# The last layer of a four-layer graph network, computed with the column nodes on the partitions

## The chip, the cores and the metric

The kernel runs on one core of a Trainium2 chip. A core has five engines that run their own instruction streams in order: TensorE (PE in the profile, with its weight loads as PEld), VectorE (DVE), ScalarE (ACT), GpSimd (POOL) and SyncE (SP), which here issues nearly all DMA transfers. The metric is the device time of one execution in microseconds (us), as the median of several runs. A profile comes from one more execution, with its own span.

## The reference

There are 16 batch elements, each with N = 1024 nodes of D = 128 features and a 1024 x 1024 adjacency matrix in fp32, sparse, with values between 0.05 and 1. Four layers follow each other, each as x = x + layer(relu(layernorm(x)), adj). The change touches the last one only, a graph attention layer:

```python
def _L3_gnn_ref(inp, A, W, a):          # inp: relu(layernorm(x)), B x N x 128
    ALPHA, NEG_INF = 0.2, -1e12
    Wh = jnp.matmul(inp, W)
    Wh1 = jnp.matmul(Wh, a[:H, :])       # one number per row node
    Wh2 = jnp.matmul(Wh, a[H:, :])       # one number per column node
    A_ = A + jnp.eye(N)
    e = (Wh1 + jnp.swapaxes(Wh2, 1, 2)) * A_
    e = jnp.where(e >= 0, e, ALPHA * e)
    scores = jnp.where(A_ > 0, e, NEG_INF)
    attention = jax.nn.softmax(scores, axis=2)
    h_prime = jnp.matmul(attention, Wh)
    return jax.nn.elu(h_prime)
```

Layers 0 and 1 average over neighbours; layer 2 scores each edge by a small network. They stay as they are.

## The kernel before

Three "lanes" of work are woven into each other: the edge network of layer 2 for batch b (the main part), the first layers of batch b+1, and the end of batch b-1 (the last update of layer 2 and the whole of layer 3). Each lane is a generator that says with every yield how much of its work is done, and `weave` advances the lane that is furthest behind. The compiler then orders the instructions of each engine. P is 128, T = 8 blocks of 128 nodes, HALF = 512.

```python
            self.work, self.lane = work, lane
            self.homes, self.home = [(f"h{lane}", n_scratch)], 0
            self.psum, self.banks, self.turn_of = psum, banks, 0
        # ...
        def scratch(self, name):
            tag, bufs = self.homes[self.home % len(self.homes)]
            self.home += 1
            return self.work.tile([P, T, P], F32, tag=tag, name=name, bufs=bufs)
        # ...
        def one(self, name):

            tag, bufs = self.banks[self.turn_of % len(self.banks)]
            self.turn_of += 1
            return self.psum.tile([P, HALF], F32, tag=tag, name=name, bufs=bufs)

        def halves(self, name):

            for h in range(NH):
                ps = self.one(f"{name}_{h}").rearrange("p (t d) -> p t d", d=P)
                yield range(h * Q, (h + 1) * Q), ps
```

A lane draws its PSUM tiles with `one`; lane c, which runs layer 3, has a single bank (`own = {"m": ("pre", 2), "a": ("a", 1), "c": ("c", 1)}`), one row buffer (`N_ROW`) and five scratch tiles (`N_SCRATCH`). The helpers for products:

```python
        def by_node(self, hT, w, name):

            for ts, ps in self.halves(f"bn_{name}"):
                for i, t in enumerate(ts):
                    nc.tensor.matmul(ps[:, i], hT[:, t], w, start=True, stop=True)
                yield slice(ts[0], ts[-1] + 1), ps

        def by_feature(self, hT, w, dst, name):

            for ts, ps in self.halves(f"bf_{name}"):
                sl = slice(ts[0], ts[-1] + 1)
                nc.tensor.matmul(ps, w, hT[:, sl], start=True, stop=True)
                nc.scalar.activation(dst[:, sl], ps, AF.Copy)

        def neighbours(self, mat, z, name):

            ps = self.one(f"nb_{name}")[:, :D]
            for k in range(T):
                nc.tensor.matmul(ps, mat[:, k], z[:, k], start=(k == 0), stop=(k == T - 1))
            return ps
```

Layer 3, with the row nodes on the partitions. For each block of 128 rows it loads the rows of adj, forms the scores, takes the exponential, turns the 128 x 1024 weights by eight transposes on PE, copies them out of PSUM, and multiplies them by wh:

```python
        def layer3(self, xt, row, name):

            hT = self.pre_ln(xt, f"3_{name}")
            yield 6
            wh = self.scratch(f"wh_{name}")
            for sl, ps in self.by_node(hT, w3_sb, f"wh_{name}"):
                nc.scalar.activation(wh[:, sl], ps, AF.Copy)
            whT = self.scratch(f"whT_{name}")
            self.by_feature(hT, w3_sb, whT, f"whT_{name}")
            ps = self.one(f"wh1_ps_{name}")
            for t in range(T):
                nc.tensor.matmul(ps[:, t : t + 1], whT[:, t], a3_sb[:, 0:1], start=True, stop=True)
            wh1 = self.small([P, T], "wh1", f"wh1_{name}")
            nc.vector.tensor_copy(wh1, ps[:, :T])
            wh2 = self.scratch(f"wh2_{name}")
            self.by_feature(whT, a2_bc, wh2, f"wh2_{name}")
            wh2 = flat(wh2)
            yield 8

            o = self.scratch(f"o3_{name}")
            rsum = self.small([P, 2, T], "rsum", f"rsum_{name}")
            for t in range(T):
                at = row(t)
                own = at[:, t * P : (t + 1) * P]
                nc.vector.tensor_add(own, own, ident)
                e = flat(self.scratch(f"e_{name}_{t}"))
                nc.vector.scalar_tensor_tensor(
                    e, wh2, wh1[:, t : t + 1], at, op0=OP.add, op1=OP.mult
                )
                self.weights(e, at, rsum[:, 0, t : t + 1], f"{name}_{t}")
                attT = self.scratch(f"attT_{name}_{t}")
                for ks, ps in self.halves(f"attT_ps_{name}_{t}"):
                    for i, k in enumerate(ks):
                        nc.tensor.transpose(ps[:, i], e[:, k * P : (k + 1) * P], ident)
                    nc.scalar.activation(attT[:, ks[0] : ks[-1] + 1], ps, AF.Copy)
                hp = self.neighbours(attT, wh, f"3_{name}_{t}")
                nc.vector.reciprocal(rsum[:, 1, t : t + 1], rsum[:, 0, t : t + 1])
                nc.scalar.activation(o[:, t], hp, AF.Copy, scale=rsum[:, 1, t : t + 1])
                yield 5
            self.sums_seen(rsum, name)
            # ... elu and the addition to xt
```

In the main path `weights` is this (sums are taken beside the mask, without the maximum):

```python
        def weights(self, e, at, total, name):
            nc.vector.scalar_tensor_tensor(e, e, L3_ALPHA, e, op0=OP.mult, op1=OP.max)
            nc.scalar.activation(e, e, AF.Exp)
            nc.vector.scalar_tensor_tensor(
                e, at, 0.0, e, op0=OP.is_gt, op1=OP.mult, accum_out=total
            )
```

Where the rows come from, and how accumulators of layer 2 are started by a product with zeros:

```python
        def acc(self, h, name):

            ps = self.psum.tile([P, HALF], F32, tag=f"acc{h}", name=name)
            nc.tensor.matmul(ps, self.zero16, self.iota2, start=True, stop=True)
            return ps
        # ...
        def last(self, s, b):


            def row(t):
                return flat(
                    self.load(
                        "c", adj[b, t * P : (t + 1) * P, :].rearrange("p (k n) -> p k n", n=P),
                        f"a3_{b}_{t}",
                    )
                )

            lane = self.c
            new = lane.scratch(f"y_{b}")
            for h, dst in enumerate(self.halves_of(new)):
                xT, msgT = self.halves_of(s.pairs[h])
                self.back(xT, s.xT[h])
                yield from lane.update(L - 1, s.xf[h], xT, msgT, dst, f"{b}_{L - 1}_{h}")
            xt = self.back(self.work.tile([P, T, D], F32, tag="x", name=f"xb_{b}"), s.x)
            nc.vector.tensor_add(xt, xt, new)
            yield from lane.layer3(xt, row, f"{b}")
            nc.sync.dma_start(out[b].rearrange("(t p) d -> p t d", p=P), xt)
```

The first layers write the transposed adjacency of each batch to DRAM, for layer 1 and the edge network:

```python
            s.adjT = self.dram.tile([N, N], F32, tag="adjT", name=f"adjT_{b}")
            # ... for each t: load rows, transpose on PE, copy
                nc.sync.dma_start(self.columns(s.adjT, t), turned)
```

Of the kernel before, what the change touches and what calls it, by code (L numbers as in the profile page):

```python
# [9 lines left out]
F32 = mybir.dt.float32  # L10
# [31 lines left out]

MAIN_US = 243.0
FIRST_US = 118.0
LAST_US = 79.0


SPLIT = (0, 1, 0, 0, 1, 0, 1, 0)
# [3 lines left out]
def tile_four_gnn_layers(  # L52
# [88 lines left out]

    half_neg = const.tile([P, T], F32, name="half_neg")
    nc.vector.memset(half_neg, -0.5)
    a2_bc = const.tile([P, P], F32, name="a2_bc")

    slide = const.tile([P, L, 2 * G - 1], F32, name="slide")
    nc.vector.memset(slide, 0.0)
# [9 lines left out]
    def fold_weights():  # L157


        nc.vector.tensor_copy(a2_bc, a3_sb[:, 1:2].to_broadcast([P, P]))  # L160
        signs = slide[:, :, G - 1]
        nc.scalar.activation(signs, we2_sb, AF.Sign)
        nc.vector.tensor_mul(we2_sb, we2_sb, signs)
        nc.vector.tensor_mul(be1_sb, be1_sb, we2_sb)
        nc.scalar.activation(we2_rows, we2_rows, AF.Abs)
        for l in range(L):
            nc.vector.tensor_mul(
                we1_sb[:, l], we1_sb[:, l], we2_rows[:, l, None, :].to_broadcast([P, 2, D])
            )


    unit = const.tile([P, 2, L], F32, name="unit")

    def scale_layer(i):
        for l in range(L):
# [3 lines left out]
    def flat(t):  # L179
        return t.rearrange("p t d -> p (t d)")  # L180
# [4 lines left out]
    class Layers:  # L185
# [8 lines left out]
        def scratch(self, name):  # L194
            tag, bufs = self.homes[self.home % len(self.homes)]
            self.home += 1
            return self.work.tile([P, T, P], F32, tag=tag, name=name, bufs=bufs)

        def small(self, shape, tag, name):
            return self.work.tile(shape, F32, tag=f"{tag}{self.lane}", name=name)  # L200
# [155 lines left out]
            nc.vector.tensor_add(dst, dst, over_t(rows["beta"][:, l], Q))  # L356
            yield 1

        def weights(self, e, at, total, name):

            nc.vector.tensor_scalar(at, at, 0.0, L3_NEG, op0=OP.is_le, op1=OP.mult)
            nc.vector.scalar_tensor_tensor(e, e, L3_ALPHA, e, op0=OP.mult, op1=OP.max)
            nc.vector.tensor_add(e, e, at)
            nmax = self.small([P, 1], "nmax", f"nmax_{name}")
            nc.vector.tensor_reduce(nmax, e, axis=AX.X, op=OP.max, negate=True)
            nc.scalar.activation(e, e, AF.Exp, bias=nmax, accum_out=total)

        def sums_seen(self, rsum, name):
            pass

        def layer3(self, xt, row, name):

            hT = self.pre_ln(xt, f"3_{name}")
            yield 6
            wh = self.scratch(f"wh_{name}")
            for sl, ps in self.by_node(hT, w3_sb, f"wh_{name}"):
                nc.scalar.activation(wh[:, sl], ps, AF.Copy)
            whT = self.scratch(f"whT_{name}")
            self.by_feature(hT, w3_sb, whT, f"whT_{name}")
            ps = self.one(f"wh1_ps_{name}")  # L380
            for t in range(T):
                nc.tensor.matmul(ps[:, t : t + 1], whT[:, t], a3_sb[:, 0:1], start=True, stop=True)
            wh1 = self.small([P, T], "wh1", f"wh1_{name}")
            nc.vector.tensor_copy(wh1, ps[:, :T])
            wh2 = self.scratch(f"wh2_{name}")
            self.by_feature(whT, a2_bc, wh2, f"wh2_{name}")
            wh2 = flat(wh2)
            yield 8

            o = self.scratch(f"o3_{name}")  # L390
# [6 lines that stand above are left out]
                nc.vector.scalar_tensor_tensor(  # L397
                    e, wh2, wh1[:, t : t + 1], at, op0=OP.add, op1=OP.mult
                )
                self.weights(e, at, rsum[:, 0, t : t + 1], f"{name}_{t}")  # L400
                attT = self.scratch(f"attT_{name}_{t}")
                for ks, ps in self.halves(f"attT_ps_{name}_{t}"):
                    for i, k in enumerate(ks):
# [3 lines that stand above are left out]
                nc.vector.reciprocal(rsum[:, 1, t : t + 1], rsum[:, 0, t : t + 1])  # L407
                nc.scalar.activation(o[:, t], hp, AF.Copy, scale=rsum[:, 1, t : t + 1])
                yield 5
            self.sums_seen(rsum, name)  # L410
            neg = self.scratch(f"neg_{name}")
            nc.vector.tensor_scalar(neg, o, 0.0, None, op0=OP.min)
            nc.scalar.activation(neg, neg, AF.Exp)
            nc.vector.scalar_tensor_tensor(o, o, 0.0, neg, op0=OP.max, op1=OP.add)
            nc.vector.scalar_tensor_tensor(xt, o, -1.0, xt, op0=OP.add, op1=OP.add)
# [26 lines left out]
    class Batch:  # L442
# [2 lines left out]

        builds = iter(())

    class Lane(Layers):

        fine = None

        def weights(self, e, at, total, name):
            nc.vector.scalar_tensor_tensor(e, e, L3_ALPHA, e, op0=OP.mult, op1=OP.max)
            nc.scalar.activation(e, e, AF.Exp)
            nc.vector.scalar_tensor_tensor(
                e, at, 0.0, e, op0=OP.is_gt, op1=OP.mult, accum_out=total
            )

        def sums_seen(self, rsum, name):

# [7 lines left out]
    class Edges:  # L470
# [25 lines left out]
        def acc(self, h, name):  # L496

            ps = self.psum.tile([P, HALF], F32, tag=f"acc{h}", name=name)
            nc.tensor.matmul(ps, self.zero16, self.iota2, start=True, stop=True)
            return ps  # L500

        def constants(self):
            con = self.con
# [40 lines left out]
        def scaled(self):  # L544

            con = self.con
            fold_weights()
            self.scale_terms()
            self.slide = con.tile([P, L, 2 * G - 1], F16, name="slide16")
            nc.vector.tensor_copy(self.slide, slide)  # L550

# [97 lines left out]
        def first(self, b):  # L649
# [5 lines left out]
            yield 8  # L655


            s.adjT = self.dram.tile([N, N], F32, tag="adjT", name=f"adjT_{b}")
            has = self.work.tile([P, len(BUCKETS), P], FP8, tag="has", name=f"has_{b}", bufs=1)
            deg = self.work.tile([P, 2, T], F32, tag="deg", name=f"deg_{b}")  # L660
            rdeg = deg[:, 1]
# [452 lines left out]
        def last(self, s, b):  # L1114


            def row(t):
                return flat(
                    self.load(
                        "c", adj[b, t * P : (t + 1) * P, :].rearrange("p (k n) -> p k n", n=P),  # L1120
                        f"a3_{b}_{t}",
                    )
                )

            lane = self.c
            new = lane.scratch(f"y_{b}")
# [3 lines left out]
                yield from lane.update(L - 1, s.xf[h], xT, msgT, dst, f"{b}_{L - 1}_{h}")  # L1130
            xt = self.back(self.work.tile([P, T, D], F32, tag="x", name=f"xb_{b}"), s.x)
            nc.vector.tensor_add(xt, xt, new)
            yield from lane.layer3(xt, row, f"{b}")
            nc.sync.dma_start(out[b].rearrange("(t p) d -> p t d", p=P), xt)

        def run(self):
# [166 lines left out]
    with tc.If(full > 0):  # L1303
        with ExitStack() as stack:
            path = Pairs(stack)
            scale_layer(1)
            with tc.For_i(0, B, 1) as b:
                path.batch(b)

# [31 lines left out]
```

## Time and profile before

| | |
|---|---|
| median of 3 runs | 5564.11 us (5563.31 to 5570.9) |
| profiled span | 5577.4 us, 115653 instructions |
| ACT busy, instructions | 3225.1 us, 7014 |
| POOL busy, instructions | 174.0 us, 137 |
| moved by DMA | 554.68 MB, mean 99 GB/s |
| loads of adjacency rows for layer 3 | 128 of 512 KB, 3.6 us to landing |

The profile counts an engine as busy while an instruction of it runs. For PE the end of a matmul is modelled, so its busy share is not a share of its peak. A group line of the profile gives the line of the kernel, the engine, the operation, the tiles (out<-in), the shapes, the count, then busy time and mean length of one, then the idle time of the engine just before such instructions and what ended it. The chain is found by going back from the last instruction, at each step to what released it.

### The profile page before, as it was taken

Reading aid. Unit: us, or ns where it says so; the run is one execution under the profiler, and the core shown is the slowest. Engines: PE = TensorE matmul, PEld = TensorE weight load, DVE = VectorE, ACT = ScalarE, POOL = GpSimd, SP = SyncE. Lnnn points to the kernel's source line nnn. Section 1 sums busy time; section 2 is a strip of 40 time slices with the busy share of each in tenths; the row PEclk is TensorE's granted clock in tenths of the full one; section 3 lists DMA queues with packets and bytes.
Section 4 is the critical chain, followed back from the end, with each engine's and each line's share of the span. In section 5 each row is a group of like instructions: output and inputs, shape, how many; then the busy total and the mean of one; then the engine's idle time right before and its main releaser. Section 6 shows DMA issues by size and latency. Waiting matters only on the chain.

```text
span 5577.4 us, 115653 instructions
## 1 busy us (share of the span) xinstructions
PE 5156.6 (92%) x46146; PEld 3845.1 (69%) x46146; DVE 4260.5 (76%) x10517; ACT 3225.1 (58%) x7014; POOL 174.0 (3%) x137
## 2 busy tenths in 40 slices
PE   5999999999999999999999999999999999999996
PEld 4676767667677676677767677676766767777665
DVE  3776787877778787787877878678787877878776
ACT  4555564755647555575655647556475665656543
POOL 0000000000000000000000000000000000000000
PEclk8999999999999999999999999999999999999998
DMA  5243324243242433424233242432424334242121
GB/s 174 62 139 93 114 69 136 81 122 97 83 131 66 123 99 96 125 62 129 92 110 110 65 137 82 116 103 79 137 68 124 95 93 132 62 129 88 47 68 41
DMA packets 706355, 554.68 MB, mean 99 GB/s; under 512 B 31248, under 2 KB 636176, under 8 KB 705808
## 3 DMA queue, kind: packets, MB, share of 16 engines
q1 hardware_dynamic: 700704, 545.57, 33.0%
q8 instruction: 364, 5.96, 0.4%
q10 hardware_dynamic: 5104, 1.65, 0.1%
q14 instruction: 183, 1.50, 0.1%
HBM read 446.44 MB, written 100.66 MB: 98 GB/s over the span
## 4 chain that ended last, share of the span: by engine, by line
PE 65%; DVE 16%; ACT 7%; DMA 6%; issue 3%; POOL 3%; SPq 1%; ACTq 0%; POOLq 0%; DVEq 0%
PE pre L916 16%; PE nb L275 9%; PE p L1027 7%; PE msg L1044 6%; DVE val L1005 5%; PE sc L948 4%; PE h L329 3%; PE bb L283 3%; DMA at<-in_adj_dram 3%; PE pn L747 2%; PE pq L780 2%; DVE hid L933 2%; POOL st L230 2%; PE attT_ps L404 2%; PE pm L747 2%
## 5 line engine op out<-in xcount | busy, mean ns | idle before, releaser
L933 DVE SCALAR_TENSOR_TENSOR hid<-pre,hid 128x320 f16<-128x320 f32 (+1 forms) x2048 | 997.4, 505 | 352.6 <-ACT hid L932 342.5
L932 ACT ACTIVATE hid<-pre 128x320 f16<-128x320 f32 (+1 forms) x2048 | 911.2, 453 | 597.2 <-PE pre L916 563.1
L916 PEld LDWEIGHTS <-part 128*128 128x128 f16 x8192 | 753.4, 99 | 411.5 <-issue 198.4
L916 PE MATMUL pre<-on,part 128*128 128x320 fp8e4 (+1 forms) x4096 | 978.9, 311 | 59.6 <-DVE hid L933 55.1
L916 PE MATMUL pre<-om,part 128*128 128x320 fp8e4 (+1 forms) x4096 | 985.4, 310 | 0.0
L1044 PE MATMUL msg<-upd,xf 128*128 128x128 f32 (+3 forms) x3008 | 613.0, 322 | 3.0 <-DVE upd L1035 3.0
L1005 DVE TENSOR_TENSOR val<-onT,u 128x384 f32<-128x384 fp8e4 (+1 forms) x1152 | 609.7, 580 | 5.0
L1027 PE MATMUL p<-val,omT 128*128 128x128 f16 x6528 | 545.5, 219 | 9.2 <-DVE val L1005 7.8
L1027 PEld LDWEIGHTS <-omT 128*128 128x128 fp8e4 x6528 | 443.3, 97 | 67.7 <-issue 18.4
L1005 DVE TENSOR_TENSOR val<-omT,u 128x384 f32<-128x384 fp8e4 x896 | 438.2, 549 | 0.0
L1044 PEld LDWEIGHTS msg<-upd,xf 128*128 128x128 f32 x3008 | 417.7, 191 | 16.3 <-DVE upd L1035 4.2
L791 ACT ACTIVATE om<-pm 128x320 fp8e4<-128x320 f32 (+1 forms) x576 | 268.1, 465 | 243.1 <-PE pm L747 241.1
L1035 DVE SCALAR_TENSOR_TENSOR upd<-p,adj 128x512 f32<-128x512 f32 x512 | 348.6, 681 | 74.1 <-PE p L1027 73.3
L1027 PE MATMUL p<-val,onT 128*128 128x128 f16 x4480 | 364.4, 219 | 1.3 <-DVE upd L1035 1.3
L969 ACT ACTIVATE srow<-sc,be_s,down 128x128 f32<-128x128 f32 (+2 forms) x512 | 255.9, 539 | 171.4 <-PE sc L948 171.0
L777 ACT ACTIVATE onT<-pn 128x384 fp8e4<-128x384 f32 (+1 forms) x576 | 296.7, 515 | 96.4 <-PE pn L747 78.9
L1027 PEld LDWEIGHTS <-onT 128*128 128x128 fp8e4 x4480 | 299.5, 97 | 52.1 <-issue 20.6
L275 PE MATMUL nb<-wh,attT 128*128 128x128 f32 x2048 | 290.6, 284 | 10.7 <-ACT attT L405 10.4
L784 DVE TENSOR_TENSOR omT<-pq,odd_off 128x384 fp8e4<-128x384 f32 x448 | 247.8, 553 | 63.5 <-PE pq L780 59.0
L275 PEld LDWEIGHTS nb<-wh,attT 128*128 128x128 f32 x2048 | 256.1, 194 | 39.5 <-ACT attT L405 25.3
L948 PE MATMUL sc<-hid,slide 128*32 128x320 f16 (+1 forms) x4096 | 271.5, 319 | 12.3 <-DVE hid L933 10.4
L734 ACT ACTIVATE far<-iota_off,mid 128x384 f16<-128x384 f16 x448 | 270.7, 616 | 13.2 <-DVE on L738 11.7
(218 smaller groups left out, 8572.5 us busy)
## 6 DMA issues: line engine op xcount, KB each, us to landing
at<-in_adj_dram SPq DMA_DIRECT2D x128, 512.0 KB, 4.1
ct<-in_adj_dram SPq DMA_DIRECT2D x128, 512.0 KB, 4.5
adjT<-tn SPq DMA_DIRECT2D x128, 512.0 KB, 5.0
l<-adjT SPq DMA_DIRECT2D x128, 512.0 KB, 3.9
a<-in_adj_dram SPq DMA_DIRECT2D x128, 512.0 KB, 3.6
adj<-adjT SPq DMA_DIRECT2D x256, 256.0 KB, 3.2
adj<-adjT SPq DMA_DIRECT2D x448, 64.0 KB, 2.1
adj<-adjT SPq DMA_DIRECT2D x192, 128.0 KB, 2.7
```

The lines of the kernel that those rows point to most:

```text
L275: nc.tensor.matmul(ps, mat[:, k], z[:, k], start=(k == 0), stop=(k == T - 1))
L734: nc.scalar.activation(far[:, : ck * P], self.iota[t == u][:, : ck * P], AF.Abs, bias=s.mid[:, i : i + 1])
L777: nc.scalar.activation(onT, pn[:, : ck * P], AF.Copy, saturate=False)
L791: nc.scalar.activation(om, pm[:, :c], AF.Copy, saturate=False)
L916: nc.tensor.matmul(pre[:, :c], path.parts[node // Q][:, k, node % Q, v], hot[:, :c], start=(hot is on and k == 0), stop=(hot is om and k = ...
L932: nc.scalar.activation(hid[:, 0, :c], pre[:, :c], AF.Relu)
L933: nc.vector.scalar_tensor_tensor(hid[:, 1, :c], pre[:, :c], 0.0, hid[:, 0, :c], op0=OP.max, op1=OP.subtract)
L948: ins = nc.tensor.matmul(self.sc[g * G : (g + 1) * G, : self.c], self.path.slide[:, self.l, G - 1 - r : 2 * G - 1 - r], self.hid[self.done ...
L1005: nc.vector.tensor_tensor(pair[:, i % 2, :ck], right[:, :ck], v.to_broadcast([P, ck, P]), op=OP.mult)
L1027: nc.tensor.matmul(self.ps[d][:, i], left[:, k], halves[:, k, :, h], start=(k, h) == terms[0], stop=(k, h) == terms[-1],)
L1035: nc.vector.scalar_tensor_tensor(upd, self.ps[d], S_SCALE, self.adj[:, d * Q : (d + 1) * Q], op0=OP.add, op1=OP.mult,)
L1044: nc.tensor.matmul(self.msg[h][:, (lo - h * Q) * P : (hi - h * Q) * P], self.xf[mb // Q][:, mb % Q], up, start=False, stop=True, skip_grou ...
```

## The change

The last layer is turned around. The column nodes stand on the partitions instead of the row nodes, and the adjacency comes from the transposed copy in DRAM that the first layers have written. So the weights have the shape that a product needs, with the summed index on the partitions, and need no transposes and no copies out of PSUM. Rows are taken in three groups of 3, 3 and 2 blocks (`L3_ROWS`), and for each group the columns in pairs of blocks: a strip is 2 x 128 columns by 384 or 256 rows. The products for the blocks of a group add up side by side in one PSUM bank, which is zeroed first by a product with zeros. Row sums, which are now sums over partitions, come from a column of ones that wh gets as its 129th column. And the score terms are computed from h and the small vectors w3 a3 (prepared once, `v3`), without the turned product whT. The transposed copy in DRAM is kept for one batch longer (`bufs=3`). The weight of the lane in `weave` goes from 79 to 75.

The core of the diff; what is cut is the preparation of constants, the fallback path that keeps the old order (it is taken only when a limit is exceeded), and names:

```diff
-LAST_US = 79.0
+LAST_US = 75.0
...
+        def score_terms(self, hT, i, name):
+            ps = self.one(f"whc_ps_{name}")
+            for t in range(T):
+                nc.tensor.matmul(ps[:, t : t + 1], hT[:, t], v3[:, i : i + 1], start=True, stop=True)
+            col = self.small([P, T], "wh1", f"whc_{name}")
+            nc.vector.tensor_copy(col, ps[:, :T])
+            row = self.scratch(f"whr_{name}")
+            self.by_feature(hT, v3_bc, row, f"whr_{name}")
+            return col, flat(row)
...
-        def weights(self, e, at, total, name):
-            nc.vector.scalar_tensor_tensor(e, e, L3_ALPHA, e, op0=OP.mult, op1=OP.max)
-            nc.scalar.activation(e, e, AF.Exp)
-            nc.vector.scalar_tensor_tensor(
-                e, at, 0.0, e, op0=OP.is_gt, op1=OP.mult, accum_out=total
-            )
+        def layer3(self, xt, strip, zero, name):
+            hT = self.pre_ln(xt, f"3_{name}")
+            yield 6
+            wh = self.wide(f"wh_{name}")
+            nc.vector.memset(wh[:, :, D : D + 1], 1.0)
+            for sl, ps in self.by_node(hT, w3_sb, f"wh_{name}"):
+                nc.scalar.activation(wh[:, sl, :D], ps, AF.Copy)
+            wh2, wh1 = self.score_terms(hT, 1, name)
+            yield 6
+
+            o = self.scratch(f"o3_{name}")
+            rsum = self.small([P, 2, T], "rsum", f"rsum_{name}")
+            for lo, hi in L3_ROWS:                      # ((0, 3), (3, 6), (6, 8))
+                n = hi - lo
+                sums = self.one(f"hp_{name}_{lo}")[:, : n * (D + 1)]
+                zero(sums)
+                sums = sums.rearrange("p (t d) -> p t d", d=D + 1)
+                for k in range(0, T, 2):
+                    at = strip(k, lo, hi)
+                    e = flat(self.scratch(f"e_{name}_{lo}_{k}"))[:, : 2 * n * P]
+                    e = e.rearrange("p (k n) -> p k n", k=2)
+                    for i in range(2):
+                        if lo <= k + i < hi:
+                            own = at[:, i, (k + i - lo) * P : (k + i + 1 - lo) * P]
+                            nc.vector.tensor_add(own, own, ident)
+                        nc.vector.scalar_tensor_tensor(
+                            e[:, i], wh1[:, lo * P : hi * P], wh2[:, k + i : k + i + 1], at[:, i],
+                            op0=OP.add, op1=OP.mult,
+                        )
+                    nc.vector.scalar_tensor_tensor(e, e, L3_ALPHA, e, op0=OP.mult, op1=OP.max)
+                    nc.scalar.activation(e, e, AF.Exp)
+                    nc.vector.scalar_tensor_tensor(e, at, 0.0, e, op0=OP.is_gt, op1=OP.mult)
+                    for i in range(2):
+                        for t in range(n):
+                            nc.tensor.matmul(
+                                sums[:, t], e[:, i, t * P : (t + 1) * P], wh[:, k + i, : D + 1],
+                                start=False, stop=True, skip_group_check=True,
+                            )
+                    yield 1.2 * n
+                nc.vector.tensor_copy(rsum[:, 0, lo:hi], sums[:, :, D])
+                nc.vector.reciprocal(rsum[:, 1, lo:hi], rsum[:, 0, lo:hi])
+                for t in range(n):
+                    nc.scalar.activation(
+                        o[:, lo + t], sums[:, t, :D], AF.Copy, scale=rsum[:, 1, lo + t : lo + t + 1]
+                    )
...
-            s.adjT = self.dram.tile([N, N], F32, tag="adjT", name=f"adjT_{b}")
+            s.adjT = self.dram.tile([N, N], F32, tag="adjT", name=f"adjT_{b}", bufs=3)
...
-            def row(t):
-                # ... load("c", adj[b, t * P : (t + 1) * P, :] ...)
+            def strip(k, lo, hi):
+                n = (hi - lo) * P
+                at = flat(self.row("c", f"a3_{b}_{lo}_{k}"))[:, : 2 * n].rearrange("p (k n) -> p k n", k=2)
+                nc.sync.dma_start(
+                    at, s.adjT[k * P : (k + 2) * P, lo * P : hi * P].rearrange("(k p) n -> p k n", p=P)
+                )
+                return at
...
+            # once, at the start: w3T by a transpose, v3 = w3 a3 by a product, v3 spread over columns
+            nc.tensor.transpose(ps, w3_sb, ident)
+            nc.tensor.matmul(ps, w3T, a3_sb, start=True, stop=True)
```

## Prediction

> **What bounds the kernel now.** I read the engine shares first, then one stretch from the middle, then the chain that ended last, and only then the groups of the last layer. The page gives busy time, share of the span and instructions:
>
> ```profile
> PE 5156.6 (92%) x46146; PEld 3845.1 (69%) x46146; DVE 4260.5 (76%) x10517; ACT 3225.1 (58%) x7014; POOL 174.0 (3%) x137
> ...
> PEclk8999999999999999999999999999999999999998
> ```
>
> TensorE (PE) leads at an almost full clock, and its row is 9 in all but the first and last slice. The busy times by stretch show that the middle is uniform:
>
> ```profile
> 2640.00:2980.00 340.00, 321.93 (x2889) 240.21 (x2888) 265.75 (x655) 201.15 (x438) 10.74 (x8) 0.98 0.34 102
> ```
>
> In 340 us PE is busy 321.9, VectorE (DVE) 265.8, ScalarE (ACT) 201.2. One batch element takes 339.2 us: in the chain the same load of xm stands at 1997.93 and, seven batches later, at 4372.49. The chain by engine:
>
> ```profile
> PE 65%; DVE 16%; ACT 7%; DMA 6%; issue 3%; POOL 3%; SPq 1%; ACTq 0%; POOLq 0%; DVEq 0%
> ```
>
> So about two thirds is PE work and most of the rest hand-offs. The last layer of batch b-1 runs woven into the main part of batch b, in 15 of 16 cases; only the last one stands alone at the end. Its groups (instructions | busy us, mean ns of one | idle before):
>
> ```profile
> L404 PE MATMUL attT_ps<-ident,e 128*128 128x128 f32 x1024 | 180.9, 282 | 36.0 <-DVE e L457 19.4 <-ACT attT L405 16.0 <-ACT o L408 0.5
> L275 PE MATMUL nb<-wh,attT 128*128 128x128 f32 x2048 | 290.6, 284 | 10.7 <-ACT attT L405 10.4
> L405 ACT ACTIVATE attT<-attT_ps 128x512 f32<-128x512 f32 x256 | 151.2, 594 | 89.8 <-PE attT_ps L404 88.8
> L397 DVE SCALAR_TENSOR_TENSOR e<-wh,wh,a 128x1024 f32<-128x1024 f32 x128 | 163.5, 1278 | 29.4 <-ACT wh L269 14.4 <-PE attT_ps L404 13.8
> L455 DVE SCALAR_TENSOR_TENSOR e<-e 128x1024 f32<-128x1024 f32 x128 | 155.7, 1216 | 0.7
> L457 DVE SCALAR_TENSOR_TENSOR e<-a,e 128x1024 f32<-128x1024 f32 x128 | 155.7, 1217 | 25.3 <-ACT e L456 23.6
> L268 PE MATMUL bf_whT<-hT,w_sb 128*128 128x512 f32 x64 | 36.7, 656 | 0.2 <-ACT whT L269 0.2
> ```
>
> 64 transposes per batch are 1024 instructions, while 64 fp32 matmuls per batch are 2048: a matmul is two instructions, a transpose one. The means of about 280 ns are not what an instruction takes from PE. The timeline of PE shows that (start, length, count):
>
> ```profile
> 2640.35 1.88 PE L329 MATMUL h<-xm,wu_sb 128*128 128x512 f32 x4
> 2642.06 1.95 PE L275 MATMUL nb<-z,l 128*128 128x128 f32 x16
> ...
> 2644.42 0.60 PE L404 MATMUL attT_ps<-ident,e 128*128 128x128 f32 x4
> ```
>
> A length is the starts of all but one plus the modelled length of the last. L404: (0.60 - 0.273)/3 = 0.109 us per transpose. L275: (1.95 - 0.275)/15 = 0.112 us. L329, 512 wide: (1.88 - 0.592)/3 = 0.429 us. I count PE in these.
>
> **What the skill says.** "Perfetto Trace Analysis", Tensor Engine Instruction (MATMUL, LD_WEIGHTS): the profiled end is estimated from the size, not observed. The trace agrees: 273 ns shown against 109 from start to start. "FP8 and Floating Point Precision", TensorE Precision Notes: true fp32 takes 4 passes. The trace shows two instructions of 0.112 us per 128x128 matmul, 0.22 in all, and half of that for a transpose; that is why a transpose saves less than a matmul would. "VectorE: DVE Perf Modes", The TRN2 errata: a fixed cost per instruction, for an fp32 tensor_tensor (N+151)/0.96 ns. It gives 1224 at N = 1024; the trace has 1216 (L455). I use it for sizes that the trace lacks. "PSUM — Partial Sum Buffer", The four PSUM rules: a matmul with the first flag clears the accumulate bits of the whole bank. Three sums that share a bank therefore can't each start themselves, which is why the change zeroes the bank by one matmul; the kernel already does this for msg.
>
> **The change part by part, per batch.**
>
> PE, removed: the 64 transposes, 64 x 0.109 = 7.0 us; whT, 2 matmuls of two instructions, 4 x 0.429 = 1.7 us. Added: three zeroing matmuls in fp16, 387, 387 and 258 wide. L1027 (fp16, 128 wide) comes every 0.057 us, so 1032 columns are about 0.5 us. The column of ones makes 128 instructions one column longer: 128 x 0.112/128 = 0.1 us. The 64 products stay 64, and the eight score products and the broadcast of wh2 (now wh1) keep their sizes. Net: 8.7 - 0.6 = 8.1 us.
>
> PE waits, removed: transposes go into the lane's one bank, four at a time, so the second four wait for ACT's copy of the first and the products wait for the second copy. L404, L275 and the score products stood idle 36.0 + 10.7 + 4.2 = 50.9 us in all. Each such wait also hides 0.273 - 0.109 = 0.16 us behind the modelled end; with some 100 waits (42 and 22 for attT, 14 for whT, 17 for e in the answers by tile, rounded up) 16 us. 67/16 = 4.2 us. The part on e (19.4/16 = 1.2 us) stays, and comes at 12 steps instead of 8 but after a shorter chain: for 768 elements 2 x 0.62 + 0.96 + 0.83 + 0.96 = 4.0 us before the first product, against 1.28 + 1.22 + 1.06 + 1.22 = 4.8. I keep 1.5 and add 0.4 for three hand-overs of the sums' bank: net 4.2 - 1.9 = 2.3 us.
>
> DVE: today 8 x (0.283 + 1.278 + 1.216 + 1.217 + 0.081 + 0.152) = 33.8 us. Afterwards the same 8192 columns in more pieces. The formula gives 0.557 at 384 and 0.424 at 256; L397 stands 0.06 over L455, so 16 x 0.62 + 8 x 0.48 = 13.8. The other two: 8 x 0.957 + 4 x 0.691 = 10.4 each. Own blocks 2.3, copies, reciprocals and memset 1.1. Sum 38.0, so +4.2 us; about a third of it overlaps the next instruction. DVE goes to some 270 of 329 us, 82%: close, still beside PE.
>
> ACT: less 16 x 0.594 + 2 x 0.587 = 10.7 us, plus about 0.6 for twelve exponentials instead of eight. It was not the bound; it answers other waits sooner.
>
> DMA: strips of 384 or 256 KB twelve times, instead of 512 KB eight times: the same 4 MB, at a share of 0.34. The lane has one row buffer, so each strip still waits for the mask of the one before.
>
> Sum for the 15 woven batches: 15 x (8.1 + 2.3) = 156 us of PE time. Not all becomes time, since 35% of the chain is not PE and DVE grows: I take 85%, 133 us. The lone last layer at the end: its loop runs from 5522 to 5568, 46 us, and in its timeline a row's DVE work is some 4.1 us, its PE part 8 x 0.11 + 16 x 0.112 = 2.7 us plus two copies. Without the transposes, copies and whT I give it 10 us. The extra start (one transpose, one product, two copies) costs about 2. In all 133 + 10 - 2 = 141, so 5564 - 141 = 5423; I say 5420.
>
> **Rivals.** (1) DVE or its hand-offs take over. For it: DVE is 16% of the chain and rises 4 us per batch while PE falls, and its pieces carry waits on ACT in twelve places instead of eight. Against it: 59 us of slack per batch. If it eats half of the gain: about 5490. (2) The queue of loads. SyncE issues in order; its own waits show 549.8 us in 62 waits for L457, the mask that frees the row, up to 45.0 at once, and loads of at stand with 3% in the chain. Twelve strips may hold other loads back more often: +2 us per batch makes 5450; if the shorter hold helps, 5390. (3) Waits dissolve fully: ACT, 10 us lighter, also shortens ACT's waits on pre (L932, 563.1 us idle) and DVE's on hid (342.5). Then 14 us per batch come, about 5345. (4) The gain is hidden because other lanes set the pace: then nothing, 5560. Against it speaks PE's row of nines. Also the order of all lanes is laid out anew by a compiler that models the times, which can move a point either way.
>
> **Range and chances.** The centre is 5420, 2.6% down. Rivals 1 and 3 set the range: 5345 to 5490. Two per cent is 5453, inside it, some 0.6 of a standard deviation above the centre: faster 0.71, same 0.25, slower 0.04.
>
> **What would show it.** Right: no attT_ps or attT group; PE instructions down by some 1024 + 64; the strips' products still 2048 instructions at 0.112 from start to start (129 wide); ACT busy down by about 160 us, DVE up by 40 to 70; the batch period at 329 to 331 us; the lone tail about 10 us shorter. Wrong: products of 129 columns clearly slower than of 128; PE idle before the strips' products of more than 70 us; DVE or loads with a clearly larger share of the chain; or a period that falls by less than 5 us although PE's work fell by 8.

## The result and the profile after

The changed kernel takes 5527.88 us (median of 4 runs, 5517.87 to 5535.55), the kernel before 5567.5 us beside it. The ratio is 0.9925, with a 95% interval of 0.9904 to 0.9947: a gain of some 40 us that is clear of the noise, where 144 were forecast. 5527.88 lies above the forecast range.

The page after, engine shares and the chain by engine:

```profile
PE 5037.3 (91%) x45109; PEld 3719.3 (67%) x45109; DVE 4304.6 (78%) x10759; ACT 3054.6 (55%) x6790; POOL 184.9 (3%) x137
...
PE 47%; DVE 27%; DMA 9%; ACT 9%; issue 4%; POOL 3%; SPq 0%; ACTq 0%; DVEq 0%; POOLq 0%
```

The busy times moved as forecast: PE -119 us, ACT -171, DVE +44. The chain changed more: PE's share of it fell from 65% to 47%, and DVE and DMA took its place (how far that belongs to the form is taken up at the end). The stretch from the middle, busy times per engine (PE, PEld, DVE, ACT, POOL), then clock, DMA share and GB/s:

```profile
2640.00:2980.00 340.00, 316.39 (x2846) 234.27 (x2846) 269.80 (x682) 191.39 (x426) 12.50 (x9) 0.99 0.35 103
```

The groups of the turned layer (instructions | busy, mean ns of one | idle before, and what ended it):

```profile
L505 PE MATMUL hp<-wh,e 128*128 128x129 f32 x2048 | 318.3, 285 | 22.3 <-DVE e L502 22.3
L496 DVE SCALAR_TENSOR_TENSOR e<-whr,whc,a 128x384 f32<-128x384 f32 (+1 forms) x384 | 210.8, 565 | 49.0 <-DMA a<-adjT 31.9 <-ACT whr L282 16.9
L502 DVE SCALAR_TENSOR_TENSOR e<-a,e 128x768 f32<-128x768 f32 (+1 forms) x192 | 165.4, 862 | 27.2 <-ACT e L501 26.3
L561 PE MATMUL hp<-iota,zero 128*128 128x387 f16 (+1 forms) x48 | 14.6, 308 | 1.2 <-ACT o L513 0.8 <-ACT whr L282 0.4
```

The products kept their number and waited little for e, and zeroing costs next to nothing. DVE now waits for strips: 31.9 us here and 4.3 at the identity blocks, 36.2 in all, where the rows of before cost 16.4 in the order that this build had. PE's timeline gives the pace of the products with 129 columns:

```profile
2658.04 1.50 PE L505 MATMUL hp<-wh,e 128*128 128x129 f32 x12
```

(1.50 - 0.275)/11 = 0.111 us: the column of ones is free.

**Where the time went.** I mark each batch by the small copy of its score terms out of PSUM. The profiled span fell by 50.8 us. Thirteen steady periods took 4407.1 us and take 4379.5: 27.6 less, 2.1 per batch. The fourteenth, in which the first layers have nothing left to do, fell from 317.4 to 298.3; the fifteenth stayed at 210, and the lone end went from 57.8 to 53.4.

To see what PE did in a steady period I counted in the trace, for each kind of PE instruction, the lowest quarter of its distances from start to start as what it occupies, and what lies above that as waiting (the sc products, four of which run side by side, count whole as occupied). Per batch:

| kernel | period | occupied | waiting |
|---|---|---|---|
| before | 339.1 | 288.3 | 50.9 |
| changed | 336.9 | 280.6 | 56.3 |

PE's work fell by 7.7 us, close to the 8.1 forecast, and its waiting rose by 5.4 where I had it fall by 2.3. After the transposes alone the kernel before waited 7.2 us per batch; those waits are gone, so some 12 us came up elsewhere. Three lines of waits (waited in total, times, longest), before:

```profile
ACT tn L669 <- DMA at<-in_adj_dram: 135.9, 74, 6.7
...
PEld L747 <- DVE omT L784: 57.2, 144, 1.2
...
PE p L1027 <- DVE val L1005: 7.8, 30, 0.3
```

and in the changed kernel:

```profile
ACT tn L739 <- DMA at<-in_adj_dram: 217.7, 86, 4.8
...
PEld L817 <- DVE omT L854: 121.1, 230, 2.1
...
PE p L1097 <- DVE val L1075: 27.7, 58, 1.2
```

They belong to the other two lanes, which the change doesn't touch. Single lines don't show that the turned form made them longer, though: with other weights in the weave ("The order", below) the first one is 203.3 to 256.7 us in the old form and 139.5 in the changed form at 79.

### The profile page after: what moved, and what is told of

The parts are those of the page before. It is cut to its first block, busy times and chain, and to the rows that moved or that the text cites. A ratio compares the mean times of both kernels' runs of the same rounds, so it can differ in the third digit from the quotient of the medians.

```text
span 5526.6 us, 113576 instructions
## 1 busy us (share of the span) xinstructions
PE 5037.3 (91%) x45109; PEld 3719.3 (67%) x45109; DVE 4304.6 (78%) x10759; ACT 3054.6 (55%) x6790; POOL 184.9 (3%) x137
## 4 chain that ended last, share of the span: by engine, by line
PE 47%; DVE 27%; DMA 9%; ACT 9%; issue 4%; POOL 3%; SPq 0%; ACTq 0%; DVEq 0%; POOLq 0%
PE pre L986 11%; DVE val L1075 10%; PE p L1097 6%; DMA at<-in_adj_dram 4%; DVE hid L1003 4%; PE nb L288 4%; PE msg L1114 4%; PE bb L296 3%; PE sc L1018 3%; DMA a<-adjT 2%; DVE omT L854 2%; PE hp L505 2%; POOL st L243 2%; PE h L342 2%; PE tn L743 2%
## 5 line engine op out<-in xcount | busy, mean ns | idle before, releaser
L986 PE MATMUL pre<-on,part 128*128 128x320 fp8e4 (+1 forms) x4096 | 966.2, 309 | 71.6 <-DVE hid L1003 60.6
L1097 PE MATMUL p<-val,omT 128*128 128x128 f16 x6528 | 534.2, 219 | 29.8 <-DVE val L1075 27.7
L505 PE MATMUL hp<-wh,e 128*128 128x129 f32 x2048 | 318.3, 285 | 22.3 <-DVE e L502 22.3
L505 PEld LDWEIGHTS hp<-wh,e 128*128 128x128 f32 x2048 | 275.5, 195 | 51.9 <-DVE e L502 29.6
L288 PE MATMUL nb<-z,ct 128*128 128x128 f32 x2048 | 279.3, 282 | 12.4 <-DMA ct<-in_adj_dram 11.9
```

What stands on the lines that cost most here:

```text
L505: nc.tensor.matmul(sums[:, t], e[:, i, t * P : (t + 1) * P], wh[:, k + i, : D + 1], start=False, stop=True, skip_group_check=True,)
L986: nc.tensor.matmul(pre[:, :c], path.parts[node // Q][:, k, node % Q, v], hot[:, :c], start=(hot is on and k == 0), stop=(hot is om and k = ...
L1097: nc.tensor.matmul(self.ps[d][:, i], left[:, k], halves[:, k, :, h], start=(k, h) == terms[0], stop=(k, h) == terms[-1],)
```

## The experiments

Theories: **P**, PE's work sets the time, and new costs of the turned form take the gain back. **D**, DVE sets the pace. **L**, the strip loads do. **O**, the order that the compiler lays out for the three lanes is good or bad by chance, and single builds carry that. Some later runs set other letters against each other; their expectations say what they stand for. All ratios are to the kernel before, run beside each.

### Parts taken away

**e1_no_turn**: the old form, without transposes and copies (the products take the unturned weights).

```diff
-                attT = ...  # eight transposes, two copies
-                hp = self.neighbours(attT, wh, f"3_{name}_{t}")
+                hp = self.neighbours(e.rearrange("p (k n) -> p k n", n=P), wh, f"3_{name}_{t}")
```

> The kernel before, with only the 64 transposes per batch and their copies out of PSUM left out (the products take the weights unturned; that part of the computation is left out). DVE work and row loads stay as before. Theory P (PE's work sets the time, and in the changed kernel the new pieces on DVE and in the loads take the gain back): 7.0 us of transposes and some 7 us of waits after them per batch go, so 90 to 190 us less, ratio to before 0.966 to 0.984. Theory D (in the woven stretch DVE and the hand-offs with it set the pace, and PE time that is taken away turns into PE waiting): the same small gain as the changed kernel, 20 to 55 us, ratio 0.990 to 0.996.

Measured: 5482.28 us, 0.9844 (0.9826 to 0.9863), 85 us less than before. Between the two, at the low edge of P. Per batch, occupied fell from 288.3 to 282.0 and waiting went from 50.9 to 51.4. So even here, with nothing added, the total of PE's waits did not fall, though the 7 us after the transposes are gone.

**e3_no_leaky**: the changed form without one DVE pass (its part of the computation is left out).

```diff
-                    nc.vector.scalar_tensor_tensor(e, e, L3_ALPHA, e, op0=OP.mult, op1=OP.max)
```

> The changed kernel without the leaky step on DVE (12 instructions of 768 or 512 columns per batch, 10.3 us of DVE; its part of the computation is left out). Theory D: DVE sets the pace, so 6 to 10 us per batch come, 90 to 160 us less than the changed kernel, ratio to before 0.963 to 0.977. Theory P or a load theory: DVE has slack, below 25 us less than the changed kernel, ratio 0.988 to 0.993.

Measured: 5473.95, 0.9827 (0.9804 to 0.985). 54 us less than the changed kernel, while DVE's busy time fell by 145 us (4304.6 to 4160.0): in neither band, somewhat over a third.

**e6_no_loads**: one strip per batch, used twelve times (eleven loads left out).

```diff
+            held = []
             def strip(k, lo, hi):
+                if not held:
+                    # take the row buffer and load this strip; later steps reuse it
```

> The changed kernel with one strip loaded per batch and used for all twelve steps (eleven of twelve loads left out). Theory L (the strip loads, through the single row buffer and the in-order SyncE queue, hold DVE and the other lanes' loads): 40 to 130 us less than the changed kernel, ratio to before 0.969 to 0.985. Theories P and D: within 20 us of the changed kernel, ratio 0.989 to 0.996.

Measured: 5479.45, 0.9838 (0.9818 to 0.9859), 48 us less than the changed kernel: in L's band.

**e5_last79**: the changed kernel with another weight in the weave.

```diff
-LAST_US = 75.0
+LAST_US = 79.0
```

> The changed kernel with the weight of its last lane in the weave back at 79: only the order of the instructions differs. If the order (theory O) decides, over 25 us either way; for the theories P, D and L within 20 us of the changed kernel, ratio to before 0.989 to 0.996.

Measured: 5550.76, 0.9969 (0.9958 to 0.998): 23 us slower than at 75, a little outside the band of the others and at the edge of O's. An edit that changes no work at all moved half as much as taking away the loads. The next runs still follow L.

### The loads and the row buffer

**e7_no_turn_no_loads**: e1_no_turn with one block of rows loaded per batch (seven of eight loads left out).

```diff
             def row(t):
+                if not held:
+                    held.append(...)   # load block t once
+                return held[0]
```

> The kernel before without the 64 transposes and their copies (as in e1_no_turn), and with one block of adjacency rows loaded per batch and used for all eight steps (seven of eight loads left out). Beside e1_no_turn (0.9844) it tells what the row loads cost in the old form. Theory N (the cost of loads is new: twelve strips through one row buffer): within 15 us of e1_no_turn, ratio to before 0.982 to 0.987. Theory S (loads cost the same in both forms, so they explain nothing of the difference): 35 to 60 us less than e1_no_turn, ratio 0.974 to 0.978.

Measured: 5463.27, 0.9808 (0.9791 to 0.9826), 19 us less than e1_no_turn: between the two bands, nearer to N's.

**e8_two_strips**: two strip buffers.

```diff
-N_ROW = {"m": 2, "a": 2, "c": 1}
+N_ROW = {"m": 2, "a": 2, "c": 2}
-MORE_OFF = 4
+MORE_OFF = 2
-            return self.work.tile([P, T, P], F32, tag=f"row{v}", ...)
+            return self.work.tile([P, 6 if v == "c" else T, P], F32, tag=f"row{v}", ...)
+            self.rows_of["a"] = "amam"      # first layers of batch 0: without lane c's buffer
```

> The changed kernel with two buffers of 3 KB for strips instead of one of 4 KB (room for it from two fewer spare tiles of the hot tables; the first layers of batch 0 use four row buffers instead of five). If the cost of loads comes from the single buffer, so that a strip can't be fetched while the one before is in use: 25 to 50 us less than the changed kernel, ratio to before 0.983 to 0.988. If it comes from the transfers themselves or from SyncE's order: within 15 us of the changed kernel, ratio 0.990 to 0.995.

Measured: 5476.1, 0.9831 (0.9814 to 0.9848), 52 us less than the changed kernel: at the edge of the first band. Why a second buffer can help is seen in the timeline of the changed kernel, a step of the last lane (start, length, engine, then what it waited for):

```profile
2629.88 0.96 DVE L502 SCALAR_TENSOR_TENSOR e<-a,e 128x768 f32<-128x768 f32 x1 [0.91 <-ACT e L501]
...
2630.87 0.36 SPq L1190 DMA_DIRECT2D a<-adjT  x1
2633.68 0.66 DVE L1003 SCALAR_TENSOR_TENSOR hid<-pre,hid 128x480 f16<-128x480 f32 x1 [2.58 <-ACT hid L1002]
2635.51 1.15 DVE L496 SCALAR_TENSOR_TENSOR e<-whr,whc,a 128x384 f32<-128x384 f32 x2 [1.16 <-DMA a<-adjT]
```

The mask ends at 2630.84, the next strip is issued at 2630.87, and DVE starts on it 4.6 us later, after it has stood idle for 1.16 us. What ended DVE's idle time on strips in the changed kernel (us, times):

```profile
  DMA a<-adjT: 36.2, 41
```

and in e8_two_strips:

```profile
  DMA a<-adjT: 14.3, 26
```

**e9_less_spare**: the side changes of e8_two_strips alone (`MORE_OFF = 2` and the `rows_of` line).

> Control for e8_two_strips: the changed kernel with its two side changes alone (two fewer spare hot tiles, four row buffers in the first layers of batch 0), still one strip buffer. If the second buffer made the gain: within 15 us of the changed kernel, ratio to before 0.990 to 0.996. If the side changes made it: near e8_two_strips, 0.981 to 0.986.

Measured: 5505.02, 0.9893 (0.9876 to 0.991): 23 us less than the changed kernel, in neither band. I had expected nothing from the side changes, and know no reason why fewer spare tiles should save time; again something that should do nothing moved it.

**e11_eight_steps**: 8 steps of 4 column blocks by 2 row blocks.

```diff
-    L3_ROWS = ((0, 3), (3, 6), (6, 8))
+    L3_ROWS = ((0, 2), (2, 4), (4, 6), (6, 8))
-                for k in range(0, T, 2):
+                for k in range(0, T, 4):       # and 4 for 2 in the strip and the inner loops
-                    yield 1.2 * n
+                    yield 2.4 * n
```

> The changed kernel with eight steps of four column blocks by two row blocks (1024 columns on DVE, 512 KB a strip) instead of twelve of two by three. DVE work about equal (32 score instructions of 256 columns, the rest in eight of 1024: some 1 us per batch less to 1 us more), still one buffer. If the number of steps, each a round of load, DVE, ACT, DVE, PE, costs the time: 20 to 45 us less than the changed kernel, ratio 0.984 to 0.989. If not: within 15 us of it, ratio 0.990 to 0.995.

Measured: 5526.85, 0.9927 (0.9909 to 0.9944), as the changed kernel: in this one order nothing speaks for the number of steps.

**e10_pool_mask**: the mask on GpSimd.

```diff
-                    nc.vector.scalar_tensor_tensor(e, at, 0.0, e, op0=OP.is_gt, op1=OP.mult)
+                    nc.gpsimd.tensor_scalar(at, at, 0.0, None, op0=OP.is_gt)
+                    nc.gpsimd.tensor_tensor(e, e, at, op=OP.mult)
```

> The changed kernel with the mask on GpSimd (a compare in place, then a product) instead of DVE: the same result, 10.4 us of DVE per batch less, and two GpSimd instructions per step. If DVE time is worth what e3_no_leaky showed and GpSimd's longer instructions lie beside other work: 30 to 55 us less than the changed kernel, ratio to before 0.982 to 0.987. If GpSimd's length in the chain of each strip outweighs it: 20 to 150 us more than the changed kernel, ratio 0.996 to 1.02.

Measured: 5645.06, 1.0132 (1.0114 to 1.0151), 117 us more than the changed kernel. Its groups:

```profile
L502 POOL TENSOR_SCALAR a<-a 128x768 f32<-128x768 f32 (+1 forms) x192 | 408.4, 2127 | 1423.7 <-DVE e L496 724.6 <-ACT part L878 251.1 <-ACT far L805 158.1
L503 POOL TENSOR_TENSOR e<-e,a 128x768 f32<-128x768 f32 (+1 forms) x192 | 315.9, 1646 | 298.0 <-issue 205.8 <-ACT e L501 56.4 <-POOL a L502 26.0
L506 PE MATMUL hp<-wh,e 128*128 128x129 f32 x2048 | 340.5, 295 | 65.6 <-POOL e L503 65.5
```

GpSimd takes 3.8 us per step for what DVE did in 0.86. The compare may lie beside the leaky step and the exponential, the product comes after them, and PE's wait for e triples. In the lone end, where no other lane runs, the longer steps are seen by themselves: it takes 68.5 us instead of 53.4.

**e12_old_two_rows**: two row buffers in the old form (`N_ROW` c = 2, `MORE_OFF = 1`, and the `rows_of` line).

> The kernel before with two row buffers for the last lane (room from three fewer spare hot tiles, four row buffers in the first layers of batch 0). The row loads cost the old form about 19 us (e7_no_turn_no_loads beside e1_no_turn), so if the single buffer hurts the turned form above all: 0 to 25 us less than before, ratio 0.9955 to 1.001. If the old form was held by it as much as the new one: 40 to 60 us less, ratio 0.989 to 0.993.

Measured: 5577.14, 1.0024 (1.0014 to 1.0034): 14 us slower, in neither band. In this one order the old form has no use for a second buffer.

### The order

**e13_two_strips_71** and **e14_two_strips_79**: e8_two_strips with only the weight changed (`LAST_US = 71.0` and `79.0`).

> e8_two_strips with the weight of the last lane in the weave at 71 instead of 75, near the sum of what its steps report. Only the order changes. From e5_last79 (23 us slower at 79 with one buffer) a shift of up to 25 us either way: ratio to before 0.979 to 0.988. If a second buffer makes the lane insensitive to its place: within 8 us of e8_two_strips, 0.9815 to 0.9845.

> e8_two_strips with the weight at 79, the weight of the kernel before. If the order costs as with one buffer (e5_last79): 15 to 30 us more than e8_two_strips, ratio 0.986 to 0.989. If a second buffer makes the lane insensitive to its place: within 8 us, 0.9815 to 0.9845.

Measured: 5409.5, 0.9723 (0.9705 to 0.9741), and 5449.01, 0.9793 (0.9776 to 0.9809). The shift is up to 67 us, beyond what I had expected, and at 79 in the other direction. This brought theory O to the front: each comparison so far was of two builds with two orders. So both forms were run with more weights. Against O stands **S**: the form decides, and the order is worth little. `LAST_US` is the only edit, in e19_two_strips_73 beside those of e8_two_strips:

**e15_old_75**, **e16_old_71**, **e20_old_83**: the kernel before.

> The kernel before with the weight of the last lane at 75 instead of 79; only the order differs. Theory O (each order of the three lanes brings its own waits, some 30 us either way, and single comparisons of two kernels carry that): anywhere within 40 us of before, ratio 0.993 to 1.007. Theory S (the old form is insensitive, the structure decides): within 8 us, 0.9985 to 1.0015.

> The kernel before with the weight at 71. Theory O: within 40 us of before, ratio 0.993 to 1.007, and not the same as at 75. Theory S: within 8 us, 0.9985 to 1.0015.

> The kernel before with the weight at 83. Theory O: within 40 us of before, ratio 0.993 to 1.007. Theory S: within 8 us, 0.9985 to 1.0015. With 71, 75 and 79 the mean of four orders of the old form.

**e17_new_71**, **e18_new_73**: the changed kernel. **e19_two_strips_73**: two buffers.

> The changed kernel (one strip buffer) with the weight at 71. Theory O: the changed kernel drew a poor order, and its form is worth more: 20 to 80 us less than at 75, ratio to before 0.978 to 0.989. Theory S (the single buffer decides): within 15 us of the changed kernel, 0.990 to 0.995.

> The changed kernel (one strip buffer) with the weight at 73. Theory O: not the same as at 71 or 75, anywhere from 0.978 to 0.997. Theory S: within 15 us of the changed kernel, 0.990 to 0.995. With 71, 75 and 79 the mean of four orders of the new form.

> Two strip buffers with the weight at 73: with 71, 75 and 79 (0.9723, 0.9831, 0.9793) the mean of four orders of that form. Theory O: anywhere between 0.970 and 0.985; mean of the four 0.976 to 0.980, and lower than the mean of the four with one buffer by more than 0.5% if the second buffer itself helps, by less if it only drew good orders.

All of them, as ratio and median us:

| weight | old form | changed form | two strip buffers |
|---|---|---|---|
| 71 | 1.0080, 5609.1 | 0.9857, 5484.1 | 0.9723, 5409.5 |
| 73 | | 0.9845, 5478.2 | 0.9815, 5466.6 |
| 75 | 0.9970, 5551.1 | 0.9925, 5527.9 | 0.9831, 5476.1 |
| 79 | 1 | 0.9969, 5550.8 | 0.9793, 5449.0 |
| 83 | 1.0174, 5667.0 | | |
| mean | 1.0056 | 0.9899 | 0.9791 |

The intervals are about 0.002 either way, so the scatter within a column is not of the measurement. O holds in every column, 2.0% in the first, 1.2% in the second, 1.1% in the third. S falls: no weight left the old form within its 8 us, and two of the three went beyond O's band as well (1.0080 and 1.0174). The mean with two strips is where O and a buffer that helps by itself had put it (0.976 to 0.980, and over 0.5% below the mean with one). And by the count of PE's time per batch:

| kernel | period | occupied | waiting |
|---|---|---|---|
| old, 75 | 338.5 | 288.4 | 50.1 |
| old, 71 | 341.6 | 288.5 | 53.1 |
| old, 83 | 346.0 | 288.9 | 57.2 |
| changed, 73 | 332.5 | 281.2 | 51.4 |
| changed, 71 | 333.4 | 280.4 | 53.0 |
| changed, 79 | 337.9 | 281.8 | 56.2 |
| two strips, 71 | 329.2 | 280.5 | 48.6 |
| two strips, 73 | 332.3 | 281.1 | 51.2 |
| two strips, 75 | 333.4 | 281.5 | 51.9 |
| two strips, 79 | 330.2 | 281.3 | 48.9 |

The split depends by up to 0.9 us on which PE instructions are taken as one kind. Occupied belongs to the form: 288.3 to 288.9, and 280.4 to 281.8. Waiting moves with the order: it spans 7 us per batch within the old form and 5 within the changed one, which is 110 and 75 us over a run. The two forms with one buffer wait equally long, 52.8 and 54.2 in the mean of four orders each, with an uncertainty of some 2 us on the difference; with two strips the mean is 50.2, and only there do orders below 50 appear.

The same waiting can be counted by the product that PE goes on to. In front of the last layer's own products the old form waits 6.9, 4.5, 5.2 and 5.7 us per batch (weights 71, 75, 79, 83), the changed form 2.1, 1.6, 1.8 and 1.8 (71, 73, 75, 79): that saving is there in every order. In front of all other products the means are 47.3 and 52.4, so 5.1 more, with an uncertainty of some 2. e1_no_turn shows the same in one order: 5.2 to 0.8, and 45.9 to 50.7. With two strips the other products wait 48.4.

The fastest kernel of all is e13_two_strips_71, 5409.5 us, faster than both. Its page:

```profile
PE 4979.5 (92%) x45109; PEld 3711.3 (69%) x45109; DVE 4297.1 (80%) x10759; ACT 3054.4 (57%) x6790; POOL 176.9 (3%) x137
```

It does the work of the changed kernel, in 118 us less. What ended DVE's idle time on strips and weights there:

```profile
  DMA a<-adjT: 15.0, 16
  ACT e L501: 10.9, 16
```

That is 15.0 against 36.2 for strips and 10.9 against 26.3 for the exponential: DVE more seldom comes too early. Both the buffer and the order differ here.

## Why the prediction was wrong

**PE's work: right.** 8.1 us per batch were forecast; 7.7 went, and in the mean of the four changed builds (281.0) against the four old ones (288.5) 7.5. The products of 129 columns run at 0.111 us, the zeroing is small. No run here tests the rule for a PSUM bank that the prediction takes from the Trainium skill: every run of the turned form zeroes the bank first.

**PE's waits, the term "4.2 - 1.9 = 2.3 us" saved: this is the step that failed.** The waits of the last layer did vanish: in front of its own products PE waits 3.8 us per batch less, in the mean of four orders of each form. But the total didn't fall, neither in this build (+5.4) nor in e1_no_turn (+0.5), which adds nothing, nor in the means (52.8 to 54.2, with an uncertainty of some 2 on the difference, where 2.3 less were forecast). I had counted a wait as time of its own. In this kernel three lanes share PE, and the waits came back in front of the other lanes' products, 5.1 us more in the means. What makes those products late stays open.

**The share of 85%: too high for the sum, about right for the work.** In the means 7.5 us less of occupied time became a period shorter by 6.1; in e1_no_turn 6.3 became 5.8. Applied to the waits as well, the share promised 8.8 us per batch, where 2.1 came in this build and 6.1 in the means.

**"A compiler that models the times, which can move a point either way": named, and then left out of the range.** This was nearly as large as all the rest of the error. At equal weights the turned form gains 125 us (71), 23 us (75) and 17 us (79); the mean of all four orders of each form differs by 1.6%, some 87 us, and the best order of each (75 and 73) by 73 us. The change as made, from 79 to 75, gains 40. So of the 104 us that are missing, some 45 lie in the orders that the two builds happened to have, by the four-order means: before stands 31 us under the mean of its form, the changed kernel 15 above its own. The rest is the form falling short of the forecast. By the scatter of the columns (51 and 35 us, each over the square root of four) this split has an uncertainty of some 30 us, and it depends on which weights are counted: the three common ones give 1.0% for the form, 56 us.

**Rival 2, the loads: nearer than I gave it credit for.** It had 2 us per batch. At the four weights tried with both, a second strip buffer, with its side changes, brings 1.3%, 0.3%, 0.9% and 1.8%, always in the same direction and 1.1% in the mean, about 60 us. The side changes alone bring 0.3% at 75; at the other weights they were not run alone. The lone end, where no other lane runs, shows the buffer by itself: 53.4 to 54.6 us with one buffer in all four orders and 53.2 with the side changes alone, 45.8 to 48.1 with two, and in the last 60 us DVE stands idle for strips 4.4 to 5.5 us with one and at most 0.9 with two. Over the whole span the wait of DVE for strips or rows (us) is less clear:

| weight | old form | changed form | two strip buffers |
|---|---|---|---|
| 71 | 37.3 | 37.4 | 15.0 |
| 73 | | 16.5 | 25.9 |
| 75 | 45.4 | 36.2 | 14.3 |
| 79 | 16.4 | 38.9 | 10.1 |
| 83 | 22.6 | | |

The one weight at which two buffers don't shorten it, 73, is the one at which they bring least. That the buffer acts by this wait in the woven stretch, rather than by giving the compiler more freedom to order, is argued and not shown. And a longer wait for loads is no mark of the turned form: the old form waits as long in two of its four orders. Whether it would gain from a second buffer over several orders was not run.

**Rival 1, DVE.** The 44 us of added work are as forecast (40 to 70), and the estimate by the formula that the Trainium skill gives for an fp32 tensor_tensor (VectorE: DVE Perf Modes, The TRN2 errata) holds: 957 ns for 768 columns, 947 in the trace (median of L502, a scalar_tensor_tensor). DVE's share of the chain did rise from 16% to 27%. But the chain moves with the order too; the old form at 83 has

```profile
PE 49%; DVE 30%; ACT 8%; DMA 6%; issue 3%; POOL 3%; SPq 0%; ACTq 0%; POOLq 0%; DVEq 0%
```

Whether DVE's time is worth a third or more of itself, as e3_no_leaky suggests, can't be told from one order; its 54 us lie within the scatter. The same holds for e6_no_loads, e7_no_turn_no_loads, e9_less_spare, e11_eight_steps and e12_old_two_rows, whose differences of 1 to 48 us I no longer read as causes. e10_pool_mask stands: 5645.1 us lies 94 above the slowest of the four orders of the changed form, with its own wait of 65.5 us in the trace.

**Rivals 3 and 4.** Neither came. The waits did not dissolve, and the gain is not hidden altogether: 87 us in the means.

**The end and the signs.** The lone end became 4.4 us shorter and not 10; its DVE work, which I had seen as its pace, grew. Of the signs listed, those on instruction counts, busy times and products came true; the period of 329 to 331 us did not (336.9). Two of those for "wrong" did come: a period that falls by less than 5 us although PE's work fell by 8, and a clearly larger share of the chain for DVE, which, as said, one order can't prove. Not foreseen were the 19 us of the fourteenth batch, where one lane runs out. It is 17 us in the means, more than the 7.5 us of work that a batch saves; why is not shown.

## What to carry to other kernels

When several lanes share engines, count a saving in the occupied time of the engine that leads, from start to start, and count removed waits as nothing until a run shows otherwise. Where a compiler lays out the order, compare two forms over several orders each, by an edit that changes no work, before a difference of one or two per cent is given a cause. The kernel one starts from has an order too: here it was a good one, and by the four-order means almost half of what was missing lay in that and in the poorer one of the changed build. And look for a stretch in which one lane runs alone: there a change shows itself without the order, as the second strip buffer did.

## What the runs showed that was not expected

- A constant that changes no work moved the time by up to 2.1%: 5551.1 us at a weight of 75 and 5667.0 at 83 in the old form, with PE's occupied time within 0.6 us per batch.
- GpSimd took 2127 ns on average for a compare of 768 or 512 columns by 128 partitions in fp32 and 1646 ns for a product, and the DVE step that runs beside it (L500) went from 861 to 986 ns on average, with single ones up to 2511 ns.
- fp32 products with 129 columns run at the pace of those with 128, 0.111 us from start to start.
